# A third buffer for gathered rows of y, and R's products spread anew over the periods

## The chip, the cores and the metric

The kernel runs on one core of a Trainium2 chip. The metric is the device time of one execution in microseconds (us). "The kernel before" is the version ahead of the change; line numbers L... in the profile are lines of that version unless the text says otherwise. The engines are PE (TensorE, matrix products), DVE (VectorE), ACT (ScalarE), POOL (GpSimd) and SP (SyncE, which here only issues DMAs). Each runs its own instructions in program order.

## The reference, cut to what matters

There are 2708 nodes with 256 features. Layer 0 is x = layernorm(x + relu([x, adj @ x] @ weight + bias)). Layer 1 mixes two chains over the result:

```python
R = S + jnp.eye(N, dtype=X.dtype)        # S is adj
R = R / R.sum(-1, keepdims=True)
Z = jnp.zeros_like(X); Xf = X; Xa = X
for n in range(STEPS):                   # STEPS = 2
    A = _top_p_attention(Xa, W1, W2, W3) # softmax of q k^T, cut to the top 0.9 of its mass
    Xf = R @ Xf
    Xa = A @ Xa
    Z = Z + Xf @ U1[n].T + Xa @ U2[n].T
h = X + Z                                # then layernorm * ln_g + ln_b
```

The output is layernorm(x + that). adj has some 0.3% of entries besides its diagonal, so in each block of 128 rows few columns are not zero.

## The kernel before, in words

**Blocks.** The 2708 rows make 22 row blocks: 21 of 128 rows, and one of 20 rows (EDGE). `rows(m)` is the height of block m.

**R's chain.** With y = X U1[1]^T and v = X U1[0]^T, the sum Xf U1 over both steps equals R (R y + v). Both are computed once and stored in device memory (`yf_d`, `v_d`). *Pass 1* (s = 0) turns v into R y + v, block by block, in `v_d`; *pass 2* (s = 1) multiplies R with that, and needs all of it, since any row may be asked for. R is never formed: for each row block m there is a list of at most 7 x 128 columns that are not zero (`ix`), the packed columns of adj for them (`adjc_d`), and the block's own 128 columns with the identity added (`own_d`). A product of R with a row block is so 8 *units*: seven with gathered rows of y or v (CC = 7), and one with the block's own rows. One unit is a product of 128 x 128 with 128 x 256, at L776, and shows as two matmul records.

**Loading a block.** `r_load(s, m)` asks for all that block m needs. `a_load` (L752, L753) brings the packed columns and own columns into a tile `adj_t` of 128 x 11 x 128, of which 8 are filled; there are three such tiles. `y_load` (L746) issues seven indirect DMAs from POOL, each of 128 rows of 256; they are the gathers. L762 brings the block's own rows of y from SP. The rows go into `yg[:, m % 2]`, one of two buffers of 8 x 256 in the memory that layer 0 used for x transposed. `r_units(n)` issues the next n units; when it begins block m it calls `r_load(s, m + 1)`. After the eighth unit the accumulator (one of two, "misc") waits for `r_out`, whose work stands two groups later in the program: in pass 1 L804 on DVE (scale by 1/row sum and add v) and a store into `v_d`, in pass 2 L819 (`arrive`).

**Step 1 of the attention.** A loop over the 22 row blocks t, of six groups g each, transposes attention weights (L561 on PE, L563 on ACT) and multiplies them with x1 (L590). Beside it the packed columns of adj are gathered by POOL (L384) and stored. The last operand of a row block's products is `x1_edge`, the edge block's rows, moved to the partitions where the last transposed columns lie. At (t, g) = (20, 2) and (20, 5) the gathers for blocks 0 and 1 of pass 1 are issued. At L993 POOL clears a few columns of a tile that it gets only when the products of L698 are done.

**Step 2 of the attention.** First some work on blocks 0 to 2 with a first stretch of R's units, `first` = 16. Then 24 *periods*, again of six groups. A period holds, for different row blocks: logits (L534) and exponentials on ACT (L871, L875), whose row maximum DVE takes (L868); searches for the threshold on ACT (L1002, L1005); the cut of a block on DVE (L1059 below_level, L1066 candidates, L1119 marks, L1124 mask); transposes and products of a masked block (L561, L563, L590); and `units[period]` units of R. R gets 8 units in periods 0 and 1, 18 in each of periods 2 to 9 (this ends pass 1), none in period 10, and 16 in each of periods 11 to 21 (pass 2).

**Finishing a block.** When both chains of a row block have arrived, it becomes a `Final`. In group 0 of a period `middle` applies the layer norm: ACT scales (L1228) into one of four `spares`, then POOL multiplies by ln_g (L1243) and adds x1 + ln_b (L1244). In group 4 of that period DVE takes the statistics of the second layer norm from it (L1218). Two blocks are so treated in a period. POOL's instructions stand in the order in which the program issues them, gathers and final operations alike.

**Memory.** Behind the two buffers in `yg`'s room lie the four `spares` and `x1_edge`. U1 has a place of its own (`c.u1`, 2 x 2 x 256 columns) and is last read when y and v are computed, before step 1. A general path, which the kernel takes only if a flag is set, reads it again.

Of the kernel before, what the change touches and what calls it, by code (L numbers as in the profile page):

```python
# [20 lines left out]
P = 128  # L21
# [18 lines left out]
ML = 16  # L40
CW, CC = 128, 7
EARLY = 12
AT = 96
# [19 lines left out]
def gnn_two_layer_kernel(ctx: ExitStack, tc: tile.TileContext, N, xT_d, x_d, adj_d, w0_d, b0_d,  # L63
# [24 lines left out]
    nc = tc.nc  # L88
    D = x_d.shape[1]
    DA = w1_d.shape[1]  # L90
    NB = (N + P - 1) // P
    DC = D // P
# [13 lines left out]

    c = Common()
    c.N, c.D, c.DA, c.NB, c.DC, c.KH, c.CHS, c.rows = N, D, DA, NB, DC, KH, CHS, rows
    c.adj_d, c.out_d = adj_d, out_d
# [21 lines left out]
    NF = 6 * NB + 4  # L131
    flags = const.tile([P, NF], FP, name="flags")
# [27 lines left out]
def fast_path(ctx, tc, c, flags, fint, xT_d, x_d, w0_d, b0_d, w1_d, w2_d, w3_d, u1_d, u2_d, g_d, b_d):  # L160
    nc = tc.nc
    N, D, DA, NB, DC, KH, CHS, rows = c.N, c.D, c.DA, c.NB, c.DC, c.KH, c.CHS, c.rows
    ident = c.ident
    adj_d, out_d, x1_d, za_d = c.adj_d, c.out_d, c.x1_d, c.za_d
    NW = SEG * NS
    NF = flags.shape[1]
# [573 lines left out]
    ready = []  # L740

    def y_load(s, m):
        y = yg[:, m % 2]
        rows_d = (c.yf_d, c.v_d)[s].rearrange("p k d -> (p k) d")
        for i in range(CC):
            nc.gpsimd.indirect_dma_start(out=y[:CW, i, :], out_offset=None, in_=rows_d,  # L746
                                         in_offset=bass.IndirectOffsetOnAxis(ap=ix[:CW, m, i:i + 1], axis=0))
        y_in[s, m] = y

    def a_load(m):  # L750
        a = adjp.tile([P, KH, P], FP, tag="adj", name="adj_t")
        nc.sync.dma_start(out=a[:CW, :CC, :].rearrange("p c i -> p (c i)"), in_=c.adjc_d[m])  # L752
        nc.sync.dma_start(out=a[:rows(m), CC, :], in_=c.own_d[m, :rows(m), :])  # L753
        a_in[m] = a

    def r_load(s, m):
        if m not in a_in:
            a_load(m)
        if (s, m) not in y_in:
            y_load(s, m)  # L760
        y = y_in.pop((s, m))
        nc.sync.dma_start(out=y[:rows(m), CC, :], in_=(c.yf_d, c.v_d)[s][:rows(m), m, :])  # L762
        r_in[s, m] = a_in.pop(m), y

    def r_units(n):
        for _ in range(n):
            s, m = r_queue[0]
            p = rows(m)
            if not r_now:
                r_now[:] = [ps_misc(), 0]  # L770
                if m + 1 < NB:
                    r_load(s, m + 1)
            acc, k = r_now
            a, y = r_in[s, m]
# [144 lines left out]
    for t in range(n_u, NB):  # L919
        u1_project(t)  # L920
    extract1(2)
    nc.vector.memset(x1_edge, 0.0)
    nc.vector.tensor_copy(x1_edge[AT:AT + rows(EDGE)], x1[:rows(EDGE), EDGE, :])
    ends = None

    at = {(m // 2, 3 * (m % 2) + 1): m for m in range(4)}
    at.update({(m - 2, 3): m for m in range(4, NB)})
    y_at = {(NB - 2, 2): 0, (NB - 2, 5): 1}
    stores = []
    blocks = {}  # L930
    for t in range(NB):
# [3 lines left out]
        if t >= NB - 3:  # L935
            b = blocks[t - (NB - 3)] = Block(t - (NB - 3))
        ra_next = finish1(t + 1) if t + 1 < NB else None
        for g in range(NG):
            turn(t, g, x1, acc, es[t % 4])
            if ends and 1 <= g <= 3:  # L940
# [471 lines left out]
def general_path(ctx, tc, c):  # L1412
# [13 lines left out]
    work = ctx.enter_context(tc.tile_pool(name="gwork", bufs=2))  # L1426
    small = ctx.enter_context(tc.tile_pool(name="gsmall", bufs=4))
    ps = ctx.enter_context(tc.tile_pool(name="gps", bufs=2, space=PSUM))

    def ps_lg():  # L1430
        return ps.tile([P, CH], FP, tag="lg", name="lg")
# [339 lines left out]
```

## Time and profile before

| | us |
|---|---|
| median of 3 runs | 1310.66 (1308.34 to 1312.3) |
| the profiled execution: its time | 1266.69 |
| its span | 1264.8 |
| granted TensorE clock, mean | 0.98 of full speed |

The profile is one execution. Its time is below that of the runs; all durations that follow are from it. The parts of its span, by the windows of the trace:

| part | from, to (us) |
|---|---|
| layer 0 and its products, y and v | 0 to 322 (last product of L677) |
| step 1 of the attention | 322 (first transposes, L561) to 725 |
| R's first units | from 726 |
| pass 1's gathers on POOL | 727 to 941 (two blocks before that, 667 to 686) |
| pass 2's gathers on POOL | 955 to 1220 |
| last instruction ends | 1265 |

Lines of the profile read so: a line of the timeline has the start in us, the duration in us, engine, line, operation, written tile <- read tiles, shapes, count; in brackets stands how long the engine was idle before and what ended that. "x1b" and "yg" are names of tiles.

### The profile page before, as it was taken

Reading aid. Unit: us, or ns where it says so; the run is one execution under the profiler, and the core shown is the slowest. Engines: PE = TensorE matmul, PEld = TensorE weight load, DVE = VectorE, ACT = ScalarE, POOL = GpSimd, SP = SyncE. Lnnn points to the kernel's source line nnn. Section 1 sums busy time; section 2 is a strip of 40 time slices with the busy share of each in tenths; the row PEclk is TensorE's granted clock in tenths of the full one; section 3 lists DMA queues with packets and bytes.
Section 4 is the critical chain, followed back from the end, with each engine's and each line's share of the span. In section 5 each row is a group of like instructions: output and inputs, shape, how many; then the busy total and the mean of one; then the engine's idle time right before and its main releaser. Section 6 shows DMA issues by size and latency. Waiting matters only on the chain.

```text
span 1264.8 us, 18701 instructions
## 1 busy us (share of the span) xinstructions
PE 1195.3 (95%) x5772; PEld 904.6 (72%) x5772; DVE 971.3 (77%) x3254; ACT 735.0 (58%) x1299; POOL 632.6 (50%) x596
## 2 busy tenths in 40 slices
PE   8999999999899999999998969999998999999885
PEld 6888878863477777777776647777766777767763
DVE  2455555784999998988851399888888999999886
ACT  2010110135566565666654498878889999989821
POOL 1000000004645552676764088788766778888850
PEclk9999999999899999999999989999999999999987
DMA  7465445434322220233233155656654645655551
GB/s 200 152 203 172 144 153 172 136 106 130 91 66 82 74 73 10 60 96 95 88 85 100 51 171 160 196 179 197 177 133 127 200 134 171 195 156 163 152 127 39
DMA packets 104248, 164.92 MB, mean 130 GB/s; under 512 B 20162, under 2 KB 76870, under 8 KB 104138
## 3 DMA queue, kind: packets, MB, share of 16 engines
q1 hardware_dynamic: 77852, 107.57, 26.4%
q0 software_dynamic: 20544, 51.17, 15.4%
q10 hardware_dynamic: 5742, 4.89, 1.3%
q8 instruction: 48, 0.79, 0.3%
q14 instruction: 62, 0.51, 0.1%
HBM read 129.66 MB, written 33.90 MB: 129 GB/s over the span
## 4 chain that ended last, share of the span: by engine, by line
PE 43%; DVE 7%; ACT 5%; DMA 4%; issue 1%; POOL 1%; POOLq 0%; ACTq 0%
PE acc L590 20%; PE misc L776 9%; PE lg L534 6%; PE tr L561 5%; DMA yg<-v_d,ix 3%; PE acc L698 2%; DMA yg<-yf_d,ix 1%; DVE e L1124 1%; PE misc L726 1%; ACT e L871 1%; DVE cand L1066 1%; DVE w L1119 1%; ACT e L1005 1%; ACT e L1002 1%; POOL yg L746 1%
## 5 line engine op out<-in xcount | busy, mean ns | idle before, releaser
L563 ACT COPY wT<-tr 128x512 f32<-128x512 f32 (+2 forms) x258 | 136.6, 537 | 205.6 <-PE tr L561 205.5
L590 PE MATMUL acc<-ya,wT 128*128 128x256 f32 x924 | 224.9, 385 | 0.0
L746 POOL DMA_INDIRECT yg<-v_d,ix x154 | 193.6, 1257 | 59.2 <-issue 25.0
L590 PE MATMUL acc<-x,wT 128*128 128x256 f32 x882 | 217.9, 387 | 0.0
L746 POOL DMA_INDIRECT yg<-yf_d,ix x154 | 186.9, 1214 | 48.3 <-issue 24.3
L274 PE MATMUL acc<-y,adj_t 128*128 128x257 f32 x924 | 206.2, 382 | 0.4 <-DMA adj_t<-in_adj 0.4
L776 PE MATMUL misc<-yg,adj_t 128*128 128x256 f32 (+1 forms) x704 | 185.6, 397 | 17.3 <-DMA yg<-v_d,ix 7.2
L590 PEld LDWEIGHTS acc<-x,wT 128*128 128x128 f32 x882 | 159.4, 190 | 58.9 <-issue 25.5
L590 PEld LDWEIGHTS acc<-ya,wT 128*128 128x128 f32 x924 | 173.6, 192 | 38.7 <-issue 16.7
L274 PEld LDWEIGHTS acc<-y,adj_t 128*128 128x128 f32 x924 | 174.9, 191 | 27.9 <-issue 1.9
L384 POOL DMA_INDIRECT adj_t<-in_adj,ix x154 | 164.9, 1071 | 51.7 <-issue 40.3
L776 PEld LDWEIGHTS misc<-yg,adj_t 128*128 128x128 f32 (+1 forms) x704 | 123.6, 190 | 65.9 <-issue 24.2
L534 PE MATMUL lg<-k,q 64*128 64x512 f32 (+3 forms) x528 | 138.5, 602 | 19.4 <-ACT e L875 7.0
L561 PE MATMUL tr<-ident,e 128*128 128x128 f32 (+1 forms) x946 | 146.0, 273 | 5.7 <-ACT wT L563 4.8
L561 PEld LDWEIGHTS tr<-ident,e 128*128 128x128 f32 (+1 forms) x946 | 118.5, 142 | 39.1 <-ACT wT L563 8.6
L351 POOL DMA_DIRECT2D part_d<-e x1 | 0.6, 573 | 274.2 <-DVE e L350 274.2
L1002 ACT ACTIVATE e<-e,st 128x2708 f32<-128x2708 f32 (+1 forms) x43 | 113.5, 2640 | 0.1
L1005 ACT ACTIVATE e<-e,st 128x2708 f32<-128x2708 f32 (+1 forms) x42 | 111.0, 2642 | 0.1
L462 ACT COPY x1T<-tr 128x256 f32<-128x256 f32 (+1 forms) x22 | 8.0, 365 | 175.9 <-PE tr L461 175.9
L596 DVE MAX8 cand<-e 128x8 f32<-128x170 f32 (+1 forms) x352 | 86.2, 317 | 14.6 <-ACT e L541 14.5
L1066 DVE MAX8 cand<-w 128x8 f32<-128x170 f32 (+1 forms) x352 | 94.3, 322 | 0.0
L534 PEld LDWEIGHTS lg<-k,q 64*128 64x128 f32 (+1 forms) x528 | 39.4, 184 | 51.4 <-issue 21.3
(247 smaller groups left out, 1742.9 us busy)
## 6 DMA issues: line engine op xcount, KB each, us to landing
adj_t<-in_adj SPq DMA_DIRECT2D x42, 704.0 KB
adj_t<-adjc_d SPq DMA_DIRECT2D x44, 448.0 KB
adjc_d<-adj_t SPq DMA_DIRECT2D x22, 256.0 KB
base<-za_d SPq DMA_DIRECT2D x40, 128.0 KB
adjc_d<-adj_t SPq DMA_DIRECT2D x22, 192.0 KB
xt<-in_x ACTq DMA_DIRECT2D x21, 128.0 KB
x_d<-x SPq DMA_DIRECT2D x21, 128.0 KB
x1b_d<-xb SPq DMA_DIRECT2D x21, 128.0 KB
```

The lines of the kernel that those rows point to most:

```text
L274: nc.tensor.matmul(acc[:p, :n], lhsT=halves[k // KH][:, k % KH, :p], rhs=y[:, k, :n], start=k == 0, stop=stop and k == NB - 1)
L384: nc.gpsimd.indirect_dma_start(out=a[:CW, i, :], out_offset=None, in_=adj_rows, in_offset=bass.IndirectOffsetOnAxis(ap=ix[:CW, m, i:i + 1] ...
L534: nc.tensor.matmul(lg[:p, h, at:at + b - a], lhsT=q[o, t * P:t * P + p], rhs=keys[s][o, i, :b - a], start=True, stop=True)
L561: nc.tensor.transpose(tr[:, k % 4, :p], columns(e[:p], k), ident[:p, :p])
L563: nc.scalar.copy(wT[:, :len(ks), :p], tr[:, :len(ks), :p])
L590: nc.tensor.matmul(acc[:p, :D], lhsT=wT[:, k % 4, :p], rhs=part_y(y, k), start=k == 0, stop=k == NB - 1)
L596: nc.vector.max(dst[:p, i * 8:(i + 1) * 8], src[:p, i * step:i * step + w])
L746: nc.gpsimd.indirect_dma_start(out=y[:CW, i, :], out_offset=None, in_=rows_d, in_offset=bass.IndirectOffsetOnAxis(ap=ix[:CW, m, i:i + 1], ...
L776: nc.tensor.matmul(acc[:p, :D], lhsT=a[:kw, k, :p], rhs=y[:kw, k, :], start=k == 0, stop=k == CC)
L1002: nc.scalar.activation(scr[:b.p, :N], e, AF.Relu, bias=b.nz, scale=b.l[k], accum_out=b.relu)
L1005: nc.scalar.activation(scr[:b.p, :N], e, AF.Sign, bias=b.nz, scale=b.l[k], accum_out=b.sign)
L1066: nc.vector.max(b.cand[:p, 8 * i:8 * i + 8], low[:p, SEG2 * i:SEG2 * (i + 1)])
```

## The change

`yg` gets three buffers of 7 x 256 (m % 3), and `r_load` is called two row blocks ahead. The own rows no longer go to `yg`; they go to two of the three unused slices of `adj_t`. The four `spares` and `x1_edge` move to the memory of U1, which the general path loads again; `x1_edge` is filled after the first threshold in the loop of step 1 instead of before the loop. Three blocks instead of two are gathered in step 1. Of R's units, 24 instead of 16 stand ahead of the periods, 16 instead of 8 in period 1, and 16 instead of 18 in each of periods 2 to 9. Pass 2 has 16 a period as before.

```diff
-    YW = 2 * (CC + 1) * D
-    yg = y_room[:, :YW].rearrange("p (s c d) -> p s c d", s=2, d=D)
-    spares = [y_room[:, YW + D * i:YW + D * (i + 1)] for i in range(4)]
-    x1_edge = y_room[:, YW + 4 * D:YW + 5 * D]
-    lists = Lists(ML, NB, flags[:, NF - 2:], yg[:, 1].rearrange("p c d -> p (c d)"))
+    YW = CC * D
+    yg = y_room[:, :3 * YW].rearrange("p (s c d) -> p s c d", s=3, d=D)
+    idle = [c.u1[:, j, i, :] for j in range(DC) for i in range(2)]
+    spares = list(idle)
+    x1_edge = idle[0]
+    lists = Lists(ML, NB, flags[:, NF - 2:], y_room[:, YW:])
...
-        y = yg[:, m % 2]
+        y = yg[:, m % 3]
...
-        y = y_in.pop((s, m))
-        nc.sync.dma_start(out=y[:rows(m), CC, :], in_=(c.yf_d, c.v_d)[s][:rows(m), m, :])
-        r_in[s, m] = a_in.pop(m), y
+        a, y = a_in.pop(m), y_in.pop((s, m))
+        own = a[:, CC + 1:CC + 1 + D // P, :].rearrange("p c i -> p (c i)")
+        nc.sync.dma_start(out=own[:rows(m)], in_=(c.yf_d, c.v_d)[s][:rows(m), m, :])
+        r_in[s, m] = a, y, own
...
-                if m + 1 < NB:
-                    r_load(s, m + 1)
+                if m + 2 < NB:
+                    r_load(s, m + 2)
...
-            nc.tensor.matmul(acc[:p, :D], lhsT=a[:kw, k, :p], rhs=y[:kw, k, :], start=k == 0, stop=k == CC)
+            nc.tensor.matmul(acc[:p, :D], lhsT=a[:kw, k, :p], rhs=y[:kw, k, :] if k < CC else own[:p],
+                             start=k == 0, stop=k == CC)
...
                 r_load(1, 0)
+                r_load(1, 1)
...
-    y_at = {(NB - 2, 2): 0, (NB - 2, 5): 1}
+    y_at = {(NB - 3, 5): 0, (NB - 2, 3): 1, (NB - 1, 1): 2}
...
-            if (t, g) == (NB - 1, 2):
-                a_load(0)
+            if t == NB - 1 and 1 < g < 4:
+                a_load(g - 2)
...
     r_load(0, 0)
+    r_load(0, 1)
...
-    first = 2 * (CC + 1)
-    units = {0: CC + 1, 1: CC + 1}
+    first = 3 * (CC + 1)
+    units = {0: CC + 1, 1: 2 * (CC + 1)}
     rest = each - first - sum(units.values())
     units.update({p: rest * (p - 1) // 8 - rest * (p - 2) // 8 for p in range(2, 10)})
     units.update({p: each * (p - 10) // 11 - each * (p - 11) // 11 for p in range(11, 22)})
```

More of the change, by code (lines that the diff above doesn't have):

```diff
@@ L108, in gnn_two_layer_kernel @@
     c.N, c.D, c.DA, c.NB, c.DC, c.KH, c.CHS, c.rows = N, D, DA, NB, DC, KH, CHS, rows
-    c.adj_d, c.out_d = adj_d, out_d
+    c.adj_d, c.out_d, c.u1_d = adj_d, out_d, u1_d
     c.x1_d = dram.tile([N, D], FP, name="x1_d")
@@ L770, in r_units @@
                 r_now[:] = [ps_misc(), 0]
-                if m + 1 < NB:
-                    r_load(s, m + 1)
+                if m + 2 < NB:
+                    r_load(s, m + 2)
             acc, k = r_now
-            a, y = r_in[s, m]
+            a, y, own = r_in[s, m]
             kw = CW if k < CC else p
-            nc.tensor.matmul(acc[:p, :D], lhsT=a[:kw, k, :p], rhs=y[:kw, k, :], start=k == 0, stop=k == CC)
+            nc.tensor.matmul(acc[:p, :D], lhsT=a[:kw, k, :p], rhs=y[:kw, k, :] if k < CC else own[:p],
+                             start=k == 0, stop=k == CC)
             r_now[1] += 1
@@ L921, in fast_path @@
     extract1(2)
-    nc.vector.memset(x1_edge, 0.0)
-    nc.vector.tensor_copy(x1_edge[AT:AT + rows(EDGE)], x1[:rows(EDGE), EDGE, :])
     ends = None
@@ L937, in fast_path @@
         ra_next = finish1(t + 1) if t + 1 < NB else None
+        if t == 0:
+            nc.vector.memset(x1_edge, 0.0)
+            nc.vector.tensor_copy(x1_edge[AT:AT + rows(EDGE)], x1[:rows(EDGE), EDGE, :])
         for g in range(NG):
@@ L1428, in general_path @@
     ps = ctx.enter_context(tc.tile_pool(name="gps", bufs=2, space=PSUM))
+    for s in range(2):
+        nc.sync.dma_start(out=u1[:, :, s, :], in_=c.u1_d[s].rearrange("(c p) e -> p c e", p=P))
     def ps_lg():
```

## The prediction, made before the changed kernel had run

> **What bounds the kernel now.** I read the page's engine shares first, then the stretches of the span (a table by windows), then POOL's and DVE's timelines over the second step, because the change touches only the products with R, and those run from 726 us on.
>
> ```profile
> PE 1195.3 (95%) x5772; PEld 904.6 (72%) x5772; DVE 971.3 (77%) x3254; ACT 735.0 (58%) x1299; POOL 632.6 (50%) x596
> ```
>
> PE is busy nearly everywhere, and POOL only half the time. That is an average over two halves. In windows of the second half (columns: window, length, busy time and count of PE, PEld, DVE, ACT, POOL, clock, DMA):
>
> ```profile
> 835.00:860.00 25.00, 25.00 (x124) 19.10 (x123) 21.47 (x75) 21.32 (x35) 20.03 (x17) 1.00 0.61 185
> 932.00:955.00 23.00, 21.96 (x105) 14.33 (x104) 20.15 (x69) 18.53 (x31) 7.06 (x9) 1.00 0.48 92
> 1045.00:1070.00 25.00, 24.36 (x120) 18.91 (x120) 24.68 (x87) 24.07 (x42) 20.71 (x19) 1.00 0.58 180
> 1190.00:1215.00 25.00, 21.02 (x97) 17.19 (x96) 21.65 (x75) 13.54 (x28) 20.72 (x19) 0.92 0.53 168
> ```
>
> POOL shows 20 of 25 us with 17 to 19 instructions. Each gather has 0.30 us of issue before it, so 17 x 0.3 = 5 us come on top: POOL is full. Its timeline says so too: from 726.86 to 941.1 and from 954.9 to 1223 there is hardly another gap than those 0.30 us.
>
> ```profile
> 940.15 0.95 POOL L746 DMA_INDIRECT yg<-yf_d,ix  x1 [0.30 <-issue]
> 954.90 0.94 POOL L746 DMA_INDIRECT yg<-v_d,ix  x1 [13.80 <-PE lg L534]
> ...
> 1017.03 2.97 POOL L746 DMA_INDIRECT yg<-v_d,ix  x1 [0.30 <-issue]
> 1022.16 0.73 POOL L1243 TENSOR_TENSOR yg<-yg,gb 128x256 f32<-128x256 f32 x1 [2.15 <-ACT yg L1228]
> ...
> 1195.66 0.74 POOL L1243 TENSOR_TENSOR yg<-yg,gb 128x256 f32<-128x256 f32 x1
> ...
> 1219.55 0.95 POOL L746 DMA_INDIRECT yg<-v_d,ix  x1 [0.30 <-issue]
> ```
>
> So a gather never waits there for a free buffer; POOL's own speed limits it. The 13.8 us between the passes are the wait for the last row block of v. DVE, full at 1045 to 1070, has a second wait, for POOL's two operations on a finished block (L1243, L1244):
>
> ```profile
> 1029.95 0.42 DVE L1218 BATCH_NORM_STATS2 bst<-yg 128x6 f32<-128x256 f32 x1
> 1197.24 0.43 DVE L1218 BATCH_NORM_STATS2 bst<-yg 128x6 f32<-128x256 f32 x1 [2.16 <-POOL yg L1244]
> 1222.08 0.43 DVE L1218 BATCH_NORM_STATS2 bst<-yg 128x6 f32<-128x256 f32 x1 [2.69 <-POOL yg L1244]
> ```
>
> It grows from nothing in period 13 to 3.5 us (2.69 + 0.84) in period 21, and is 10.6 us in all. A period of pass 2 takes DVE about 23.3 us (L1059 at 1016.15, 1039.42, 1062.69), while POOL's sets of four operations stand 24.8 us apart ((1220.51 - 1047.05)/7). POOL is the slower.
>
> **A rule against the trace.** POOL needs 1.25 us a gather (0.95 + 0.30), but 2.6 to 3.8 us for one that meets DVE's 3.05 us L1059 or L1124, two in a period, about 2.1 us lost each. [...] The trace decides: I count the locks.
>
> **The change, part by part.**
>
> *Gathers ahead.* 21 gathers instead of 14 stand ahead of POOL's 38.8 us wait at L993 (686 to 725 us), so seven move into idle time. Pass 1 after 726.86 has 133 instead of 140. At 214.2/140 = 1.53 us, POOL's last yf_d gather comes 10.7 us earlier, near 930. In pass 2 the third buffer itself gives POOL nothing, as it never waits for a buffer.
>
> *Units.* A unit is two matmul records, 0.43 us. Ahead of the loop there are 24 instead of 16, in period 1 16 instead of 8, in periods 2 to 9 16 instead of 18. The 8 up front (3.5 us) fall where PE waits for gathers until 741.2 anyway: nothing on PE; if that cover were missing, 3.5. But the "misc" accumulators are two. DVE's L804, two in a row at 733.16, become three, and the third waits for the third block, which can start only after the first L804: 733.7 + 8 x 0.43 = 737.2. What is queued behind it on DVE is the candidate search, the next maximum (L868 at 737.75), then L1124 and L1059. With one more L804 (0.4) in period 1, DVE reaches period 2 some 4.3 us late (759.9 to 764.2). Bounds: 0, if ACT (busy to 742.2) set the start, and 4.3. On PE, period 1 now needs the second block beyond, whose gathers land near 762 (757.87 plus 4.1 to landing); period 2's first transposes go from 761.65 to about 765. I take +3.3.
>
> *Pass 1.* PE's periods of 18 units take 23.1 where nothing waits (851.00 to 874.17 by L868); 24.3 and 25.0 in periods 7 and 8, where gathers are late. With 16 units, 22.3, as period 12 shows (992.06 to 1014.34). POOL gives two blocks in 14 x 1.25 + 2 x 2.1 = 21.7 to 22.2. Following gather 14p - 5 plus 4.2 us to landing, periods 2 to 4 are POOL's (period 4 near 808, against 805.7); from there PE's six at 22.3 lead to 941.8 for period 10, against 948.5. Gain 6.7; bounds 4 (only 16 units, 6.9, less 3.3) and 10.7 (POOL's).
>
> *Between the passes.* Period 10 is ACT's (24.17 of 25 us from 955 to 980); no price, it moves as a whole. POOL's start of pass 2 and DVE move by the same 6.7.
>
> *Pass 2.* The order of instructions shows 49 instead of 42 gathers ahead of the first four final operations, then 14 a period as before, 7 ahead of the last. The final operations are queued behind one more block. Without the common shift: the first set runs at 1020.3 + 8.75 = 1029.1 to 1032.1 instead of 1022.2 to 1025.2, the first L1218 (due at 1029.95) waits 0.65 for its block, the second (then due at 1031.2) 0.9: 1.6 together. DVE is then on POOL's 24.8 us from period 13 on: period 20 at 1032.1 + 7 x 24.8 = 1205.7 against 1198.7, so 7.0 late. In period 21 POOL has only 7 gathers left and DVE waits no more: DVE needs 21.2 from there, 1226.9 against 1223.6. Loss 3.3, of which 2.9 reach the last products (1232.6 against 1229.7). The PE waits for yg in pass 2 (about 9 from 1132 to 1215) go; DVE is late in their place. Bounds: 0 and 7.0.
>
> *No price.* Own rows go to a[:, 8:10] on the same SP queue with the same bytes; a_load a block earlier waits for the product just done (SP has its waits now at L762, 97 us, on the same event). x1_edge's two small operations move behind finish1(1) on DVE, under 0.6 us either way. U1 is last read before step 1, and its reload is in the branch not taken.
>
> **Sum.** 1264.8 - 6.7 + 2.9 = 1261.0 us of span, 0.3% less. The profiled execution took 1266.69 us; the runs' median is 1310.66, 3.5% above, for which no view has a reason. I carry over the ratio: 1310.66 x 1261.0/1264.8 = 1306.7. If PE is the slower one in those runs, pass 1 loses POOL's part of the gain, and it is nearer to nothing.
>
> **The rivals.**
> - *POOL bounds everything* (10.7 gained, nothing given back). For it: PE waits for yg in both passes; DVE has 3 us free in a period of pass 1. Against: PE is 25 of 25 us busy at 835. 1264.8 - 10.7 = 1254.1, or 1299.6.
> - *The final operations decide* (slower). DVE is full in pass 2; a set behind seven more gathers is 8.75 plus a lock of 2.1 late. If period 21 doesn't give back the 7.0, and pass 1 gains only 2 after its 3.3 late start, +5: 1269.8, or 1315.8. It decides from the point where what pass 2 keeps exceeds what pass 1 gained. Against: POOL's last period has half the gathers.
> - *Nothing comes of it.* The gathers are hidden or PE sets all: within 2 us, 1308.7 to 1312.7. Against: chain and waits name yg.
>
> **How the numbers follow.** 0.3% (3.9 us) is about what a measurement of this kernel can tell from no change. My own case, 52%: net -8 to +2 about -3.8, so half beyond 0.3% (26%) and half within (26%); its own range is 1302 to 1313. POOL throughout 20%, all faster. The final operations 22%, slower. Nothing 6%, same. Faster 0.46, same 0.32, slower 0.22. The range takes in most of the two outer cases: 1297 to 1317.
>
> **What would show it.** Right: 21 gathers before L993's counterpart; DVE waiting some 3.5 us for PE near 734; the last yf_d gather near 931, the first of v_d near 948 (954.9 now); DVE's wait for POOL's final operations up from 10.6 to about 14 us, from period 13 to 20 and none in 21; hardly a PE wait for yg in pass 2. Wrong: the first v_d gather no earlier than 952 (no gain in pass 1), or before 945 (POOL's case); a DVE wait over 20 us (the slower case), or under 8; sets of final operations nearer than 24 us, which would mean that POOL isn't the limit.

## The result, and the profile after

The changed kernel took 1323.81 us (median of 4 runs, 1321.67 to 1327.54), the kernel before, beside it, 1311.48 (4 runs). The ratio is 1.0112, with a 95% interval of 1.0084 to 1.014: slower by 1.1%, where I had forecast 1306.7 and a range up to 1317. The profiled execution is one of those runs: 1324.26 us, span 1322.4. Beside its span of 1264.8 in the profile of before, that is 58 us more, and only some 12 of them are the change's by the medians (15 by the ratio, which is the record's own figure and not quite the quotient of the medians, here and below). So the first thing to explain is why the runs of the kernel before are themselves 45 us longer than its profile.

Line numbers from here on are the changed kernel's. L747 is the gather, L778 the product with R, L807 r_out, L872 the next maximum (one for each period), L875 the exponentials, L1065 and L1130 DVE's two long operations, L1224 the statistics of a block, L1249 and L1250 POOL's final operations. In the kernel before they are L746, L776, L804, L868, L871, L1059, L1124, L1218, L1243 and L1244. L535, L562, L564, L591 and L999 are its L534, L561, L563, L590 and L993.

From the page after: the busy time of each engine, and the shares of the chain that ended last.

```profile
PE 1200.7 (91%) x5772; PEld 908.3 (69%) x5772; DVE 972.8 (74%) x3254; ACT 734.0 (56%) x1299; POOL 624.3 (47%) x596
...
PE 65%; DVE 16%; ACT 7%; issue 4%; another core or an unknown queue 4%; POOL 3%; DMA 1%; ACTq 0%; POOLq 0%; DVEq 0%
```

The work is the same, and PE needs only 5.4 us more for it (1200.7, 1195.3 before), so the lower mean clock (0.968, 0.98 before) doesn't make the 58 us either. Most of them are idle time, and for a part of the chain the trace has no name: "another core", on a program of one core. The table by windows shows where (columns: window, length, then busy time and count of PE, PEld, DVE, ACT, POOL, then clock and DMA):

```profile
774.00:804.00 30.00, 3.25 (x12) 1.66 (x12) 8.17 (x27) 1.68 (x3) 18.99 (x21) 0.63 0.36 106
885.00:910.00 25.00, 25.00 (x128) 19.82 (x127) 22.91 (x78) 21.78 (x37) 18.91 (x16) 1.00 0.61 182
1043.00:1068.00 25.00, 18.25 (x87) 13.67 (x85) 13.88 (x47) 15.21 (x22) 18.51 (x18) 0.87 0.55 170
```

The second row is as full as its like in the profile of before. In the first, 30 us long, PE, DVE and ACT work for 3, 8 and 2 us, and only POOL goes on with its gathers. The timeline has the waits (in brackets the idle time before an instruction, and what ended it; "remote" is an event that the trace doesn't hold):

```profile
803.31 3.61 POOL L747 DMA_INDIRECT yg<-yf_d,ix  x1 [5.22 <-remote]
803.09 1.11 ACT L875 ACTIVATE e<-lg,nmax 128x1024 f32<-128x1024 f32 x1 [28.32 <-remote]
804.35 1.47 PE L535 MATMUL lg<-k,q 64*128 64x330 f32 x4 [25.60 <-ACT e L875]
...
965.90 0.94 POOL L747 DMA_INDIRECT yg<-yf_d,ix  x1 [0.30 <-issue]
1005.77 0.94 POOL L747 DMA_INDIRECT yg<-v_d,ix  x1 [38.92 <-PE tr L562]
...
1061.13 0.38 PE L591 MATMUL acc<-ya,wT 128*128 128x256 f32 x1 [1.75 <-issue]
```

ACT's L875 waits 28.32 us for logits that PE had finished near 777; PE then waits for ACT. While that lasts, POOL issues gathers every 1.25 us, from 760.9 to 798.1, thirty of them with no pause, and then waits 5.22 us itself for an event that the trace doesn't hold. Near 1061 PE itself gets one instruction in 1.4 to 2.1 us, beside 16 gathers without a pause. And POOL, the bound of pass 1 in the profile of before, now has all gathers of yf_d out by 967 and waits 38.92 us for v (13.80 before). None of this is in my prediction, and none of it is in the profile that I predicted from.

### The profile page after: what moved, and what is told of

It is laid out like the page before. It is cut to its first block, busy times and chain, and to the rows that moved or that the text cites. A ratio compares the mean times of both kernels' runs of the same rounds, so it can differ in the third digit from the quotient of the medians.

```text
span 1322.4 us, 18670 instructions
## 1 busy us (share of the span) xinstructions
PE 1200.7 (91%) x5772; PEld 908.3 (69%) x5772; DVE 972.8 (74%) x3254; ACT 734.0 (56%) x1299; POOL 624.3 (47%) x596
## 4 chain that ended last, share of the span: by engine, by line
PE 65%; DVE 16%; ACT 7%; issue 4%; another core or an unknown queue 4%; POOL 3%; DMA 1%; ACTq 0%; POOLq 0%; DVEq 0%
PE acc L591 22%; PE acc L274 12%; PE lg L535 8%; PE tr L562 6%; PE misc L778 6%; DVE e L1130 2%; PE acc L678 2%; DVE w L1125 2%; POOL yg L747 2%; PE misc L410 2%; DVE cand L1072 2%; PE acc L699 2%; PE misc L449 1%; PE misc L727 1%
## 5 line engine op out<-in xcount | busy, mean ns | idle before, releaser
L564 ACT COPY wT<-tr 128x512 f32<-128x512 f32 (+2 forms) x258 | 135.9, 536 | 222.9 <-PE tr L562 154.2
L591 PE MATMUL acc<-x,wT 128*128 128x256 f32 x882 | 222.0, 392 | 17.6 <-ACT wT L564 11.4
L747 POOL DMA_INDIRECT yg<-v_d,ix x154 | 193.6, 1257 | 87.2 <-PE tr L562 44.5
L591 PE MATMUL acc<-ya,wT 128*128 128x256 f32 x924 | 226.2, 386 | 4.4 <-issue 4.3
L591 PEld LDWEIGHTS acc<-x,wT 128*128 128x128 f32 x882 | 161.2, 192 | 79.7 <-issue 36.0
L747 POOL DMA_INDIRECT yg<-yf_d,ix x154 | 176.2, 1144 | 67.4 <-issue 40.4
L591 PEld LDWEIGHTS acc<-ya,wT 128*128 128x128 f32 x924 | 173.5, 192 | 43.2 <-issue 21.4
L384 POOL DMA_INDIRECT adj_t<-in_adj,ix x154 | 171.3, 1112 | 51.8 <-issue 42.7
L535 PE MATMUL lg<-k,q 64*128 64x512 f32 (+3 forms) x528 | 138.6, 602 | 49.0 <-ACT e L875 27.6
L778 PE MATMUL misc<-yg,adj_t 128*128 128x256 f32 (+1 forms) x616 | 162.4, 394 | 8.4 <-issue 3.5
L562 PE MATMUL tr<-ident,e 128*128 128x128 f32 (+1 forms) x946 | 146.7, 274 | 16.4 <-DVE e L1130 8.3
L562 PEld LDWEIGHTS tr<-ident,e 128*128 128x128 f32 (+1 forms) x946 | 118.3, 142 | 52.6 <-issue 15.7
L778 PEld LDWEIGHTS misc<-yg,adj_t 128*128 128x128 f32 (+1 forms) x616 | 108.6, 190 | 49.5 <-issue 26.9
L535 PEld LDWEIGHTS lg<-k,q 64*128 64x128 f32 (+1 forms) x528 | 39.8, 184 | 81.6 <-ACT e L875 29.6
```

The costliest lines, as they stand in the source:

```text
L384: nc.gpsimd.indirect_dma_start(out=a[:CW, i, :], out_offset=None, in_=adj_rows, in_offset=bass.IndirectOffsetOnAxis(ap=ix[:CW, m, i:i + 1] ...
L535: nc.tensor.matmul(lg[:p, h, at:at + b - a], lhsT=q[o, t * P:t * P + p], rhs=keys[s][o, i, :b - a], start=True, stop=True)
L562: nc.tensor.transpose(tr[:, k % 4, :p], columns(e[:p], k), ident[:p, :p])
L564: nc.scalar.copy(wT[:, :len(ks), :p], tr[:, :len(ks), :p])
L591: nc.tensor.matmul(acc[:p, :D], lhsT=wT[:, k % 4, :p], rhs=part_y(y, k), start=k == 0, stop=k == NB - 1)
```

## The experiments

All later runs give the kernel before beside the kernel tried. They fell on six chips, and each chip shows one of two faces. On chips 3, 6, 8 and 15 the kernel before takes 1266 to 1268 us, on chips 9 and 0 it takes 1312 to 1315, as in the runs on record (whose chip isn't named). I call them prompt and late chips. Chip 3 was prompt in three sets of runs, but 9 and 0 were met in one each, so it isn't shown that the chip decides and not the time of the run. What decides is the ratio to before on the same chip.

| kernel | chip | median us (runs) | before, us (runs) | ratio, 95% interval |
|---|---|---|---|---|
| changed, on record | not named | 1323.81 (4) | 1311.48 (4) | 1.0112 (1.0084 to 1.014) |
| b_again (before) | 15 | 1272.4 (1) | 1267.52 (46) | |
| layout_only | 15 | 1267.03 (20) | 1267.52 (46) | 0.9999 (0.9989 to 1.0008) |
| old_shares | 15 | 1262.12 (11) | 1267.52 (46) | 0.9959 (0.9946 to 0.9973) |
| two_up | 15 | 1268.94 (20) | 1267.52 (46) | 1.0018 (1.0007 to 1.0029) |
| a_again (changed) | 3 | 1264.27 (14) | 1267.34 (33) | 0.9972 (0.996 to 0.9983) |
| moves_only | 3 | 1265.57 (20) | 1267.34 (33) | 0.9986 (0.9975 to 0.9996) |
| third_later | 3 | 1264.14 (12) | 1267.18 (21) | 0.9974 (0.9961 to 0.9987) |
| one_ahead_2 | 3 | 1260.85 (10) | 1267.18 (21) | 0.9956 (0.9946 to 0.9966) |
| both | 3 | 1259.81 (4) | 1267.18 (21) | 0.9951 (0.9934 to 0.9969) |
| long_run | 3 | 1263.08 (1) | 1268.05 (9) | |
| old_shares_2 | 3 | 1259.34 (4) | 1268.05 (9) | 0.9938 (0.9922 to 0.9955) |
| a_third (changed) | 3 | 1263.57 (6) | 1268.05 (9) | 0.9964 (0.9951 to 0.9976) |
| b_third (before) | 9 | 1314.69 (10) | 1314.61 (24) | 0.9993 (0.9966 to 1.002) |
| a_fourth (changed) | 9 | 1329.41 (15) | 1314.61 (24) | 1.011 (1.0088 to 1.0132) |
| spaced | 6 | 1275.74 (6) | 1267.04 (10) | 1.0059 (1.0039 to 1.0078) |
| old_shares_2b | 6 | 1260.61 (5) | 1267.04 (10) | 0.9947 (0.9921 to 0.9973) |
| one_pause | 8 | 1269.97 (6) | 1266.37 (7) | 1.0024 (1.0008 to 1.004) |
| one_pause_b | 0 | 1327.67 (2) | 1311.6 (3) | 1.0109 (1.0002 to 1.0217) |

### Is the profile of before like its runs?

The kernel before, unchanged, and the changed kernel, unchanged.

> The kernel before once more, unchanged, for the trace of a run that takes what its timed runs take. Theory (late instructions): the profile of before that the prediction was made from (span 1264.8) is not like its runs (1308 to 1313); a usual run has, like the one of the changed kernel, stretches in which instructions arrive late while POOL issues gathers without pause, some 45 us in all in steps 1 and 2. Expected: span near 1309, stretches of late instructions on ACT, DVE and PE worth 35 to 50 us, at other places than in the changed kernel or shorter. Rival (all work is slower in usual runs: clock, transfers): span near 1309 with no stretch of that kind and every period about 3.5% longer.

> The changed kernel once more, unchanged, beside the kernel before and moves_only on one chip. In the runs that gave the ratio 1.011 the kernel before took 1311; in later runs, on chip 15, it took 1267.5, as in its profile. Theory (late instructions belong to the chip or the session, not to the change): where the kernel before takes 1267, the changed kernel has no stretch of late instructions either and takes 1259 to 1265, which is faster. Rival (the change brings the late instructions, through its long runs of gathers): 1278 to 1284, with the stretches near 700, 780 and 1050 us as before.

b_again fell on a prompt chip: span 1270.6, no gap of over 0.4 us on PE, DVE or ACT without an event that ends it. So half of the theory fell: a usual run of before on that chip *is* like its profile. a_again settled the other half. Where before takes 1267, the changed kernel has no such gap either, and is faster, 0.9972. In a_again's timeline ACT's L875 waits 1.90 us where it waited 28.32:

```profile
733.41 0.48 DVE L807 SCALAR_TENSOR_TENSOR base<-misc,rinv,base 128x256 f32<-128x256 f32 x1 [1.21 <-PE misc L778]
736.99 0.48 DVE L807 SCALAR_TENSOR_TENSOR base<-misc,rinv,base 128x256 f32<-128x256 f32 x1 [3.09 <-DMA base<-v_d]
748.70 1.11 ACT L875 ACTIVATE e<-lg,nmax 128x1024 f32<-128x1024 f32 x1 [1.90 <-PE lg L535]
...
932.12 0.94 POOL L747 DMA_INDIRECT yg<-yf_d,ix  x1 [0.30 <-issue]
952.14 0.94 POOL L747 DMA_INDIRECT yg<-v_d,ix  x1 [19.08 <-PE tr L562]
...
1028.29 0.43 DVE L1224 BATCH_NORM_STATS2 bst<-u 128x6 f32<-128x256 f32 x1 [3.42 <-POOL u L1250]
1029.79 0.43 DVE L1224 BATCH_NORM_STATS2 bst<-u 128x6 f32<-128x256 f32 x1 [0.86 <-POOL u L1250]
...
1198.30 0.43 DVE L1224 BATCH_NORM_STATS2 bst<-u 128x6 f32<-128x256 f32 x1 [2.16 <-POOL u L1250]
```

The change thus has two results, one for each kind of chip. The parts were then tried on the prompt ones.

### The parts of the change on prompt chips

moves_only and layout_only gather one block ahead as before, with the new places in memory; layout_only has the new shares too (its expectation says "as before"; the kernel that ran has the new ones). Against the changed kernel:

```diff
-                if m + 2 < NB:
-                    r_load(s, m + 2)
+                if m + 1 < NB:
+                    r_load(s, m + 1)
...
-    y_at = {(NB - 3, 5): 0, (NB - 2, 3): 1, (NB - 1, 1): 2}
+    y_at = {(NB - 2, 2): 0, (NB - 2, 5): 1}
...
-    first = 3 * (CC + 1)
-    units = {0: CC + 1, 1: 2 * (CC + 1)}
+    first = 2 * (CC + 1)
+    units = {0: CC + 1, 1: CC + 1}
```

The last four lines are in moves_only alone; r_load(0, 1) and r_load(1, 1) go in both, and so does the old place of `a_load`. old_shares has only those last four lines.

> The kernel before with the moves of memory alone (own rows in adj's tile, spare tiles in U1's memory, three buffers for gathered rows in turn), but rows gathered one block ahead and units shared out as before. Theory (late instructions follow from gathers running further ahead): 1308 to 1315, as before. Rival (the memory moves cost, by another placement in SBUF or the wait of the own rows' transfer for adj's tile): 1316 to 1324.

> The kernel before with the moves of memory alone: own rows in adj's tile, spare tiles in U1's memory, three buffers in turn; one block ahead and shares of units as before. (layout_only had the new shares as well, other than its text said.) Theory (the moves cost nothing): within 0.2% of the kernel before. Rival (they cost by the SBUF placement or the own rows' transfer, which layout_only's new shares hid): 0.4% slower or more.

> The changed kernel with the old shares of units (16 ahead of the loop, 8 in period 1, 18 in periods 2 to 9); three buffers and two blocks ahead are kept. Theory (late instructions): the stretch of late instructions beside the gathers stays (the gathers are the same), so 1319 to 1327; passes of 18 units cost up to 5 more. Rival (the third product ahead of the loop is what delays period 1): 1308 to 1315.

two_up gathers two blocks, not three, in step 1:

```diff
-    y_at = {(NB - 3, 5): 0, (NB - 2, 3): 1, (NB - 1, 1): 2}
+    y_at = {(NB - 3, 5): 0, (NB - 2, 3): 1}
```

> The changed kernel with only two blocks gathered in step 1; the third block is gathered when the products begin. Theory (late instructions come with long unbroken runs of gathers): the 16 us lost at 696 to 713 shrink to those of a run of 14 gathers, but the run of gathers in period 1 is 7 longer: 1312 to 1325. Rival (the late instructions have nothing to do with the number of gathers up front): 1320 to 1328, with the stretch at 696 to 713 unchanged.

The moves of memory cost nothing (0.9986), and so do moves and shares together (0.9999). The times expected of layout_only, old_shares and two_up were those of a late chip, so the runs say nothing on their theories of late instructions; the ratios tell what each part is worth without them. With the third buffer and the third block gathered in step 1, old_shares gains 0.4%. Without that third block, two_up loses all of it (1.0018): the seven gathers ahead of POOL's long wait are worth 1.0018 - 0.9972, some 5.8 us, and the new shares without them start period 2 at 766.77 instead of 762.89 (L872). That the new shares cost something on top (old_shares 0.9959 against 0.9972) lies within the two intervals; old_shares_2 below is lower than one_ahead_2 in the same way, again within them.

### What the third r_out and the final operations cost

third_later calls the third block's r_out one slot later; one_ahead_2 goes back to one block ahead in the second pass; both has the two edits.

```diff
-                later[1].append(lambda s=s, m=m, acc=acc, base=base: r_out(s, m, acc, base))
+                later[2 if (s, m) == (0, 2) else 1].append(
+                    lambda s=s, m=m, acc=acc, base=base: r_out(s, m, acc, base))
```

```diff
-                if m + 2 < NB:
-                    r_load(s, m + 2)
+                ahead = m + 2 - s
+                if ahead < NB and (s, ahead) not in r_in:
+                    r_load(s, ahead)
```

> The changed kernel with one edit: r_out of the third block, the third in a row on DVE ahead of period 0's search, is called one slot later. In a_again's and two_up's traces period 1 begins at 741.2 (the next maximum), in those with the old shares at 738.0. Theory (the third r_out, waiting for a product that waits for the first r_out, is what delays the start): the next maximum near 738.5, 2 to 3 us less in all, 1261 to 1262.5 where before is 1267. Rival (PE's eight products more are what delays it): no change, 741 and 1264.

> The changed kernel with one edit: in the second pass a block is gathered one ahead again, after the first two, so that 42 gathers and not 49 stand before the first final operations on POOL, as in the kernel before. Theory (the final operations behind seven more gathers cost the 3.4 us that period 13 takes longer, and set periods of 24.13): period 13 back at 23.3, the second pass 141 instead of 147 us over seven periods, of which 2 to 4 reach the end: 1260 to 1262.5. Rival (POOL's speed sets the second pass, wherever the final operations stand): within 1 us of 1264.

> The changed kernel with both edits of third_later and one_ahead_2. Theory: both gains add, 1257 to 1260 where before is 1267, a ratio of 0.993 to 0.995. Rival (what the start gains is lost to POOL's rate in the second pass): as the better of the two alone, near 1261.5. Should these runs be ones with late instructions (before at 1311), the shorter unbroken runs of gathers in the second pass are expected to lose less there: 10 to 20 us under the changed kernel's 1324.

third_later's theory fell. Period 1 does begin earlier (L872 at 739.38, not 741.18), but period 2 begins at 764.10 against 762.89. In its timeline (L873 is L872 there) PE stands for gathered rows in between:

```profile
757.12 2.07 PE L778 MATMUL misc<-yg,adj_t 128*128 128x256 f32 x4 [3.11 <-DMA yg<-yf_d,ix]
764.10 0.29 DVE L873 TENSOR_REDUCE nmax<-lg 128x1 f32<-128x128 f32 x1 [1.77 <-PE lg L535]
```

From 726 to 765 us PE waits 8.2 us for gathered rows, 7.0 in a_again. What DVE saves is lost again to these waits.

one_ahead_2's theory held: 1260.85, against 1264.27 and 1263.57 of the changed kernel on the same chip. Period 13 takes 23.26 us (26.66 in a_again), the maximum of period 19 comes at 1149.10 instead of 1156.31. A line of the view of waits (us in total, times, longest) of each, first a_again from 1000 us on:

```profile
DVE bst L1224 <- POOL u L1250: 17.9, 16, 3.4
```

and one_ahead_2, whose code stands one line further:

```profile
DVE bst L1225 <- POOL u L1251: 10.7, 9, 2.7
```

DVE's waits for the final operations fall by 7.2 us. They follow this order: 17.8 to 18.0 us in all eight prompt traces with two blocks ahead in pass 2, 10.6 to 10.8 in all eight with one. Of the 7.21 us at period 19, 1.16 are there before period 13 (1007.79 against 1008.95), so pass 2 gives 6.0. Less of it reaches the end: 2.7 and 3.4 us by the medians, some 1 and 2 by the ratios (0.9956 against 0.9964 and 0.9972), whose intervals still touch. both (1259.81) isn't measurably better than one_ahead_2, as third_later's trace would have it.

old_shares_2 is one_ahead_2 with the old shares; a_third is the changed kernel beside it.

> The changed kernel with the old shares of units and with one_ahead_2's edit. Theory (the new shares cost 2 us, as old_shares against a_again says, and the order of POOL in the second pass costs 3.4): the gains add, 1258 to 1260. Rival (the new shares pay once the second pass no longer waits for POOL): as one_ahead_2, near 1261.

> The changed kernel unchanged, for a ratio beside old_shares_2 on one chip. Theory (late instructions belong to where it runs): near 1264 where before is 1267. Rival: near 1324, whatever before takes.

> old_shares_2 once more, the fastest kernel of the runs on chip 3. Where before takes 1314: Theory (the third block gathered at the end of step 1 and the run of gathers behind L999 lose there as in the changed kernel, the second pass does not): 1316 to 1324, still slower than before. Rival (the new shares start the loss in period 1, as PE frees the buffers early): 1303 to 1310, faster than before. Elsewhere 1259 again.

At 0.9938 and 0.9947 on two chips, old_shares_2 has the lowest ratio of all, about 0.6% under the kernel before where chips are prompt. It met no late chip.

### What is late on a late chip

First, whether a long run of gathers is enough. long_run adds 21 gathers into idle tiles behind step 1's 21:

```diff
                 y_load(0, y_at[t, g])
+                if y_at[t, g] == 2:
+                    more = idle[1:]
+                    for k in range(21):
+                        nc.gpsimd.indirect_dma_start(
+                            out=more[k % 3][:CW], out_offset=None, in_=c.yf_d.rearrange("p k d -> (p k) d"),
+                            in_offset=bass.IndirectOffsetOnAxis(ap=ix[:CW, k // 7, k % 7:k % 7 + 1], axis=0))
```

> The changed kernel with 21 more gathers of rows of yf_d, into three spare tiles that nothing reads before the second pass writes them, right behind the 21 gathers of step 1: in a_again POOL stands idle there from 695 to 723 us. It makes a run of some 40 gathers with hardly a pause over the end of step 1. Theory (a long unbroken run of gathers is enough to make the other engines' instructions late, as in the first trace of the changed kernel): gaps of over 0.7 us on ACT, PE or DVE that no event of the trace ends, and the memset L999's place (723.6 in a_again) 10 us or more later. Rival (the long run is not enough; the runs of 1311 and 1324 had something besides): no such gap, the end of step 1 within 2 us of a_again's.

```profile
698.03 0.95 POOL L978 DMA_INDIRECT u<-yf_d,ix  x1 [0.31 <-issue]
```

(L978 are the added gathers.) 22 gathers in a row without a pause up to 699.0, and 18 more to 728 with pauses of up to 1.8 us: no instruction is late. On a prompt chip the run of gathers is not enough. Then both kernels once more:

> The kernel before, unchanged, for a trace of it in runs where it takes 1311. Theory (it too meets late instructions there): if these runs are of that kind, about 44 us in gaps that no event of the trace ends, of which some 15 before 690 us, as in the changed kernel's first trace. Rival (its 44 us are a general slowness): no such gaps and all periods longer. If they are not of that kind, 1267 and no gap of over 0.4 us.

> The changed kernel, unchanged, beside it. If these runs are of the kind of 1311 and 1324: late instructions again at the end of step 1, in period 1 and in period 12, which would make the places belong to the program; at other places, which would make them chance. Otherwise 1264 and no gap.

They fell on chip 9, a late one, and repeat the record: before 1314.69, changed 1329.41. a_fourth's timeline:

```profile
702.04 0.95 POOL L747 DMA_INDIRECT yg<-yf_d,ix  x1 [0.30 <-issue]
702.71 0.59 ACT L564 COPY wT<-tr 128x512 f32<-128x512 f32 x1 [7.93 <-remote]
707.06 0.95 POOL L747 DMA_INDIRECT yg<-yf_d,ix  x1 [0.30 <-issue]
711.25 0.50 ACT L564 COPY wT<-tr 128x256 f32<-128x256 f32 x2 [7.96 <-remote]
773.87 1.13 PE L535 MATMUL lg<-k,q 64*128 64x512 f32 x4
795.97 0.95 POOL L747 DMA_INDIRECT yg<-yf_d,ix  x1 [0.30 <-issue]
802.12 3.60 POOL L747 DMA_INDIRECT yg<-yf_d,ix  x1 [5.21 <-remote]
801.91 1.11 ACT L875 ACTIVATE e<-lg,nmax 128x1024 f32<-128x1024 f32 x1 [28.41 <-remote]
1068.35 0.59 ACT L564 COPY wT<-tr 128x512 f32<-128x512 f32 x1 [10.50 <-remote]
```

and b_third's, of the kernel before:

```profile
708.78 0.86 ACT L563 COPY wT<-tr 128x512 f32<-128x512 f32 x2 [7.15 <-remote]
779.46 0.95 POOL L746 DMA_INDIRECT yg<-yf_d,ix  x1 [0.30 <-issue]
780.36 3.05 DVE L1124 SCALAR_TENSOR_TENSOR e<-w,st,e 128x2720 f32<-128x2720 f32 x1 [5.00 <-remote]
780.71 3.52 POOL L746 DMA_INDIRECT yg<-yf_d,ix  x1 [0.30 <-issue]
781.12 1.11 ACT L871 ACTIVATE e<-lg,nmax 128x1024 f32<-128x1024 f32 x1 [6.08 <-remote]
886.95 0.81 ACT L871 ACTIVATE e<-lg,nmax 128x660 f32<-128x660 f32 x1 [2.80 <-remote]
```

So the kernel before meets late events too, and the places are the program's own: 28.41 us at L875 in a_fourth, 28.32 in the trace on record. Against the same kernel on a prompt chip (b_again and a_again), by the next maximum of each period (for the end of step 1, the third maximum, at 687 us in b_again), the two are late by:

| at | before, us | changed, us |
|---|---|---|
| end of step 1 | 27.9 | 25.0 |
| period 1 | 26.7 | 26.7 |
| period 2 | 31.6 | 51.1 |
| period 9 | 48.8 | 53.2 |
| period 12 | 44.1 | 53.0 |
| period 13 | 47.3 | 65.6 |
| end of the span | 46.6 | 62.1 |

More than half of before's 46.6 us is lost by the end of step 1, where the two kernels differ little. The change loses 24.4 us in period 1, where before loses 4.9; in periods 2 to 9 before loses 17.2 and the changed kernel 2.2; period 12 costs the changed kernel 12.5, before 3.2. A single trace is good to some us here: b_again is 5 us above the median of its chip, and against the profile of before the 46.6 would be 52.4. By the medians of chips 9 and 3 the two kernels are late by 47 and 65 us.

What is late is the update of a semaphore, by its records in the trace. Those of PE, between 770 and 803 us of a_fourth:

```
785.00  790.60  801.82  801.87  801.91  801.95
```

PE's product that ACT waits for ended at 775.0. Four updates are recorded within 0.13 us at 801.9, 4.9 us after POOL's last gather of the run ended (796.92), and ACT starts at 801.91. In the stretch, DVE's instructions, each waiting for the one before, start at 778.03, 779.42, 782.22, 782.93, 784.33 and 787.12: in steps of 0.70 us and multiples of it. Elsewhere such an instruction follows with some 0.03 us of idle time. DVE's recorded updates from 778.01 to 798.30 lie on a grid of 0.70 us, and PE's two of 785.00 and 790.60 lie on the same one: at most one recorded update of the two engines together in 0.70 us. In the trace on record PE's 773.54, 777.79 and 788.31 lie on DVE's grid too (771.42 to 798.11), but at 777.79 an update of each is recorded.

Also, 1386 records of updates are there for 1860 of DVE and 851 for 986 of PE; in a_again 1857 and 985. The missing ones come after POOL's first indirect DMA of the program (at 285 us): before it 344 of 344 and 132 of 132 are there, and 2288 records of DMA landings (2282 in a_again), after it 5948 of a_again's 14374. b_third, one_pause_b and the trace on record (1368 of 1860, 828 of 986) lack about as many. Since records are missing, the lateness of a single update can't be had from its number, only from flushes like that at 801.9 and from the wait that ends there.

In the three places of a_fourth the last held update comes 2 to 5 us after a run of gathers has ended (708.0, 796.9 and 1066.2, by POOL's timeline). Other waits end otherwise: ACT's wait of 7.93 us ended at 702.71 inside the run that ends at 708.0, and in b_third DVE and PE were let through at 780.34 and 781.03 after 16 gathers, with no pause in POOL. The length of a run is also in part an effect: on a prompt chip a gather that meets one of DVE's long operations, and takes 2.63 to 3.76 us (a_again, 897 to 926 us), ends every run of pass 1 after 15 gathers at most (12 in the profile of before). In the stall DVE gets to none before 801.86, and POOL goes on until it has to wait itself, from 796.9.

spaced and one_pause test whether a pause does it: 14 memsets of an idle tile on POOL ahead of the gathers of blocks 4, 5 and 6, or of block 6 alone.

```diff
         y = yg[:, m % 3]
+        if (s, m) == (0, 6):
+            for _ in range(14):
+                nc.gpsimd.memset(idle[1], 0.0)
```

> The changed kernel with 14 small memsets of an idle tile (about 4.4 us of POOL by L968's 0.31 us each) ahead of the gathers of blocks 4, 5 and 6 in the first pass, so that the run of 30 gathers from 760 to 797 us is broken twice or more. On chip 9 the changed kernel lost 27 us there: PE's semaphore update of 775.0 is recorded only at 801.8, 4.9 us after the last of those gathers. Theory (a run of gathers without pause holds back the other engines' semaphore updates, and a pause of 4 to 5 us lets them through): where the kernel before takes 1314, 10 to 22 us less than the changed kernel's 1329; elsewhere (before 1267) 2 to 8 us more than its 1264, for POOL's lost time. Rival (the updates are late by their place in the program, not by the gathers): slower than the changed kernel in both kinds of runs.

> The changed kernel with one pause: 14 small memsets of an idle tile (4.4 us of POOL) ahead of block 6's gathers in the first pass, which stand at 782.2 in the changed kernel's trace of chip 9, in the middle of its run of 30 gathers. Theory (a run of gathers without pause holds back the other engines' semaphore updates, and the pause lets them through): where the kernel before takes 1314, PE's updates of about 775 are recorded near 786 and not at 801.8, and the changed kernel's 1329 falls by 8 to 20. Rival (the updates are late by their place in the program): they stay late until near 802, and the time is 1329 to 1335. Where before takes 1267: 1264 to 1268, for the pause alone.

> one_pause once more. Where the kernel before takes 1314, Theory (the unbroken run of gathers holds the semaphore updates back): PE's updates of about 775 recorded near 786 and not at 801.8, and 8 to 20 us less than the changed kernel's 1329. Rival (late by their place in the program): late until near 802, and 1329 to 1335. Where before takes 1267: 1270 again, and the question stays open.

spaced and one_pause met prompt chips, where they took 8.7 and 3.6 us more than before, and more than I had expected for the pauses (1275.74 and 1269.97, against 1266 to 1272 and 1264 to 1268). one_pause_b met a late one, chip 0:

```profile
784.46 0.95 POOL L750 DMA_INDIRECT yg<-yf_d,ix  x1 [0.30 <-issue]
785.40 5.22 POOL L747 MEMSET u<- 128x256 f32 x14
788.60 1.11 ACT L878 ACTIVATE e<-lg,nmax 128x1024 f32<-128x1024 f32 x1 [11.21 <-remote]
789.86 1.47 PE L535 MATMUL lg<-k,q 64*128 64x330 f32 x4 [9.56 <-ACT e L878]
...
847.92 0.81 ACT L878 ACTIVATE e<-lg,nmax 128x660 f32<-128x660 f32 x1 [4.72 <-remote]
861.54 0.29 DVE L875 TENSOR_REDUCE nmax<-lg 128x1 f32<-128x128 f32 x1 [8.15 <-remote]
```

(This kernel's code stands three lines further: L878 the exponentials, L875 the next maximum, L750 the gathers; L747 are the memsets.) PE's updates are recorded up to 770.86, then none until six at 788.41 to 788.64, 3.0 us into the pause. ACT's wait is 11.21 us instead of 28.41. The updates come in the pause and 13 us earlier than at the same place of a_fourth. That speaks for POOL's gathers and against the place in the program, in one trace. The total didn't follow: 1.0109 against 1.011, from two runs, with an interval from 1.0002 to 1.0217. From the maximum of period 1 to that of period 2 it takes 34.1 us (46.1 in a_fourth), but from period 3 to 4 35.9 (24.6): POOL now issues 15 gathers without a pause from 832.4 to 850.9, and DVE and ACT wait there and just behind (ACT's 4.72 us end at 847.92, inside that run). Twelve us are saved in one place and eleven lost in the next, so my expectation of 8 to 20 us less failed, while the stall behaved as its theory said.

## Why the prediction was wrong

**The sum was right where its profile is.** 1261.0 us of span were predicted; on chip 3 it is 1261.8 (a_again) and 1262.8 (a_third), and 0.997 was the ratio, which came out as 0.9972 and 0.9964. The ratios decide here: two traces of before are 5.8 us apart (1264.8 and 1270.6), more than the 3.8 forecast.

**The step that failed** is the last of the sum: "The profiled execution took 1266.69 us; the runs' median is 1310.66, 3.5% above, for which no view has a reason. I carry over the ratio". That made the 44 us a property of all work, which the change leaves alone: its effect on them was put at nothing. The traces show waits for late events in their place, 46.6 us for the kernel before on chip 9, 62.1 for the changed one. By period 2 the changed kernel has lost 19.5 us more, by period 9 4.4, by period 13 18.3, at the end 15.5, against the 3.8 that it was to gain. That the change does this by the order of POOL's gathers is what the places and one_pause_b point to; it isn't shown beyond these. I had the discrepancy in hand and no trace of a run of that kind; without one, no term of the sum could have held it, but the range should have been wider for it, on the slow side above all.

**Gathers ahead, right in kind.** 21 gathers stand ahead of the long wait, and pass 1's last gather begins at 932 (931 predicted). two_up shows them to be worth 5.8 us.

**Units, right.** Period 2 begins at 762.89 (763.2 predicted); DVE's waits at L807 are 1.21 and 3.09 us (3.5 predicted for PE; the longer one is put down to the base's transfer). Of the two causes that I named, PE's wait for gathered rows is left; DVE's third L804 isn't one, since third_later, which moves it away, starts period 2 no earlier (764.10).

**Pass 1, right in rate, not settled in sum.** PE's periods of 16 units take 22.29 us (22.3 predicted), but PE waits 10.1 us for gathered rows from 740 us on, 9.1 of them before 790, and period 10 begins 2.7 to 7.6 us earlier than in the two prompt traces of before (943.96 against 946.70 and 951.52), below and above the 6.7 predicted. By the ratio the gain is a little smaller: one_ahead_2, whose pass 2 has the old order, is 0.44% or 5.6 us under before. The first gather of v comes at 952.14 in a_again and 951.41 in a_third, 948 predicted. I had called 952 or later a sign of no gain; that was set too close, since in before it comes at 954.90 or, in b_again, at 959.71.

**Pass 2, right.** 49 gathers of v stand ahead of the first final operations on POOL in the trace on record, 42 in the profile of before, as the program issues them. Period 20 was to be 7.0 late; one_ahead_2 against a_again gives 6.0 by period 19. 2.9 of it were to reach the end; 1 to 3.4 do, by ratio or median. The waits come at once, 3.42 in period 13, then 0.8 to 0.9 twice a period, 2.16 once in period 20, to 17.9 (14 predicted). PE's waits for v's rows are gone, as predicted (2.3 us against 11.9 in b_again, for the weight loads).

**Gathers beside DVE's long operations.** I had counted the gathers that meet L1059 or L1124 at the 2.6 to 3.8 us that they take in the profile of before (the locks). They are there in a_again too. In pass 2 its sets of final operations stand 24.14 us apart (1050.85 to 1074.99); 14 gathers at 1.25 and four operations at 0.76 are 20.5, and the two gathers that met L1130 and L1065, 2.60 and 2.96 us instead of 0.95, are the rest. That such gathers take longer is measured; why they do, no run here shows.

**The rivals.** The slower one was right in mechanism on every prompt chip (the final operations do cost DVE) and wrong in size: it gave 1315.8, and this cost is 1 to 3.4 us in a kernel that still gains. What made the runs on record slower was no rival of mine. Of the signs that I named, DVE's wait for the final operations, over 20 us for the slower case, was in the slower trace not even there until period 17: POOL had caught up while the others stood. Its 5.0 us in all fall under my sign "under 8", which I had given no case.

**Still open.** Why chips 9 and 0 are late and 3, 6, 8 and 15 are not; what ties the late updates to the gathers; why records are missing on late chips alone, and only once gathers have begun; whether the writing of the profile's own records has a part in the stall, since every trace here holds such records. And old_shares_2 on a late chip wasn't tried.

## What to carry to other kernels

If the profile and the timed runs of one kernel differ by more than the change can bring, get a trace of a run that takes what the runs take before you size anything: the missing time has places, and an edit may move them. A queue of POOL with no pause isn't only a throughput: on two of six chips here (9 and 0) the other engines' events were late beside it, by up to 27 us in a_fourth, so a version that gathers further ahead should be measured on more than one chip. Where a buffer is added to run ahead, look at what is queued behind the transfers on the issuing engine, and go back to the old order there.

## What the hardware showed that I had not expected

- The same two kernels stand at 0.997 to each other on chip 3 (0.9972 and 0.9964), and at 1.011 on chip 9 and on record (1.011 and 1.0112).
- On late chips updates of semaphores are recorded up to 27 us late beside indirect DMAs that are issued every 1.25 us without a pause, and records go missing from the first such DMA on (1386 of DVE's 1860 are there in a_fourth). The longest waits ended 2 to 5 us after the run of gathers or 3.0 us into a pause, others inside a run. 22 gathers without a pause did nothing of the kind on chip 3.
- While it lasts, single instructions of DVE start in steps of 0.70 us, and PE's and DVE's recorded updates share one grid of that step (a_fourth, 778.01 to 798.30 us). Near 1061 us on record PE's instructions, which wait for nothing that the trace shows, start 1.41 or 2.1 us apart (1061.13, 1063.24, 1064.65, 1066.75), two or three such steps.
